# Turning tiles by blocks on a trip through device memory instead of on TensorE

## The chip, the cores and the metric

The kernel runs on one core of a Trainium2 chip. The metric is the device time of one execution in microseconds; lower is better. A core has five engines that run their own instruction streams in order: TensorE (PE in the profile; its weight loads are listed as PEld), VectorE (DVE), ScalarE (ACT), GpSimd (POOL) and SyncE (SP). In this kernel SP issues all DMAs. The engines wait for each other through semaphores.

## The reference

The input is x of 4 sequences of 512 tokens with 512 features. Two blocks are added to it one after the other.

The first is gated linear attention with 4 heads of 128 on the normalised x:

```python
x = x + attn(layernorm(x))
# attn, by chunks of 128 tokens and by heads:
#   k = k / max(norm(k), 1e-12)
#   decay[c, e] = exp(cla[c] - cla[e]) where e <= c, else 0
#   scores = (q @ k.T) * beta * decay ;  y_local = scores @ v
#   y = y_local + (q @ state) * exp(cla)
#   state = state * exp(cla_end) + (k * beta * exp(cla_end - cla)).T @ v
x = x + ffn(layernorm(x))
# ffn: weights of 4 bits with a scale for 32 values,
#   gate = h @ Wg.T ; up = h @ Wu.T ; out = (gelu(gate) * up) @ Wd.T
```

All of it is in fp32. In the second block the kernel splits each fp32 operand into a high and a low part and a mixed one, and multiplies the three parts.

## The kernel before, in words

A tile is 128 tokens by 512 features in fp32, one row to a partition: 256 KB. A sequence has 4 tiles (n = 0 to 3), each of them also a chunk of the attention, so chunks run from (0,0) to (3,3). TensorE contracts over partitions, so a normalised tile must be turned (features onto partitions) before it is multiplied with weights, and so must k before the scores.

The program is a list of steps p. For each sequence b there are 12: four products of v (`product_v`), four of q, four of k. After each product `behind(p)` issues other work by p modulo 3, and by it a chunk of the attention takes three steps, 9 steps behind its sequence: chunk 4b+n begins at p = 9 + 3(4b+n).

- p%3 == 0: `chunk_lead` (kT, the turned k, into which ScalarE copies the bank), `chunk_decay` (exponentials on ScalarE, masks and products on GpSimd, the next load of sums, `load_sums`).
- p%3 == 1: `turn("f")` and `turn("a")` turn what the second and the first norm have left over; then `chunk_scores`: the scores `sp` out of kT and q, and VectorE's product with the decay (L597). Then the loads of x and of xr, the residual.
- p%3 == 2: `chunk_sums`: `dp` and `yp`, then VectorE's residual sum (L649); then `rest`: GpSimd's `chunk_values`, `second_norm` of the chunk and the sum of the state; then `first_norm` of a tile of the next sequence; then `settle`, which normalises what is waiting (L312, `hn_f` and `hn_a`).

`norm` takes the statistics on VectorE, the power -0.5 on GpSimd (`rs`), and defers the rest to `settle`. `turn` makes four TensorE transposes of 128x128 into a PSUM bank (L333) and calls `use`: for the first norm ScalarE copies the bank into hT, the input of the products; for the second ScalarE makes the high part (L356), VectorE the low and the mixed one (L357, L358), and three stores bring them to device memory, from where the second block loads them.

The order is written out by hand: each engine runs its instructions in the order in which these functions issue them, and so does SP with its DMAs. From step 13 on, a slot of `unpack` (VectorE's conversion of the 4-bit weights) follows each step with p%3 of 1 or 2. The second block begins at step 46 and drives the remaining chunks from inside its own products. The functions that the diff touches, and `turn`, which it no longer uses for some tiles, are below. `one_k` hands out the SBUF places of 2 KB a partition and takes them back.

Of the kernel before, what the change touches and what calls it, by code (L numbers as in the profile page):

```python
# [8 lines left out]
F32 = mybir.dt.float32  # L9
# [4 lines left out]
AF = mybir.ActivationFunctionType  # L14
ALU = mybir.AluOpType
# [6 lines left out]
P = 128  # L22
# [13 lines left out]
def f32(t):  # L36
    return t.bitcast(F32)
# [3 lines left out]
def tile_gated_linear_attention__then__nvfp4_geglu(  # L41
# [19 lines left out]
    nc = tc.nc  # L61
    B, T, D = x.shape
    H = D // P
    NCH = T // P
    NT = B * NCH
    KC = D // P
# [59 lines left out]
    def heads(t):  # L126
        return t.rearrange("p (h d) -> p h d", d=P)

    def bc(a):
        return a.unsqueeze(2).to_broadcast([P, a.shape[1], P])  # L130
# [161 lines left out]

    settled, turned = [], []

    def norm(src, key, use, parts=1, within=None):

        st = small.tile([P, 6], F32, tag="st", name=f"st_{key}")
        nc.vector.bn_stats(st, f32(src))
        if within:
            within()  # L300
        mv = small.tile([P, 2], F32, tag="mv", name=f"mv_{key}")
        nc.vector.bn_aggr(mv, st)
        rs = small.tile([P, 1], F32, tag="rs", name=f"rs_{key}")
        nc.vector.tensor_scalar(rs, mv[:, 1:2], 1e-5, None, ALU.add)
        nc.gpsimd.tensor_tensor(rs, rs, minus_half[:, :1], ALU.pow)

        def settle():

            hn = one_k.get(f"hn_{key}")
            w = D // parts  # L310
            for cols in (slice(i * w, (i + 1) * w) for i in range(parts)):
                nc.vector.tensor_scalar(  # L312
                    f32(hn)[:, cols].rearrange("p (c two j) -> p c two j", two=2, j=P),
                    f32(src)[:, cols].rearrange("p (c j two) -> p c two j", two=2, j=P),
                    mv[:, 0:1], rs, ALU.subtract, ALU.mult,
                )
            one_k.put(src)
            turned.append((hn, key, use))

        settled.append(settle)  # L320
# [6 lines left out]
    def turn(which, most=NT):  # L327
        for done in [t for t in turned if t[1][0] in which][:most]:
            turned.remove(done)
            hn, key, use = done  # L330
            tp = psum(f"tp_{key}")
            for k in range(KC):
                nc.tensor.transpose(tp[:, k * P : (k + 1) * P], f32(hn)[:, k * P : (k + 1) * P], ident)  # L333
            one_k.put(hn)
            use(tp)

    def first_norm(b, n, src, within=None):
        if n == 0:
            hT[b] = [two_k.get(f"hT{b}_{c}") for c in range(KC // 2)]

        soon = b == n == 0

        def use(tp):
            for c in range(KC // 2):
                to = f32(hT[b][c])[:, :, n * P : (n + 1) * P]
                new = tp[:, 2 * c * P : 2 * (c + 1) * P].rearrange("p (two t) -> p two t", two=2)
                for part in ((0, 1), (1, 2)) if soon else ((0, 2),):
                    nc.scalar.copy(to[:, slice(*part), :], new[:, slice(*part), :])

        norm(src, f"a{b}_{n}", use, 2 if soon else 1, within)  # L350

    def second_norm(b, n, src):
        def use(tp):
            g = [one_k.get(f"g{j}_{b}_{n}") for j in range(3)]
            hi, lo, mi = g
            nc.scalar.activation(hi, tp, AF.Copy, scale=HI)  # L356
            nc.vector.tensor_tensor(lo, tp, f32(hi), ALU.subtract)  # L357
            nc.vector.scalar_tensor_tensor(mi, f32(hi), ONE_E, tp, ALU.mult, ALU.subtract)  # L358
            for j in range(3):
                nc.sync.dma_start(  # L360
                    h2d[b][j][:, :, n * P : (n + 1) * P].rearrange("k p t -> p k t"), heads(f32(g[j]))
                )
            one_k.put(*g)

        norm(src, f"f{b}_{n}", use)


    zs, ss = {}, {}
# [25 lines left out]
    def product_q(b, h):  # L394
# [10 lines left out]
            f32(q_sb[b][h // 2])[:, h % 2, :], pq, AF.Identity, bias=bq_sb[:, h : h + 1]  # L405
        )

    def product_k(b, n):

        pk = psum(f"pk_{b}_{n}")  # L410
        for k in range(KC):
            nc.tensor.matmul(  # L412
                pk, f32(hT[b][k // 2])[:, k % 2, n * P : (n + 1) * P], f32(wk[k // 2])[:, k % 2, :],
                start=(k == 0), stop=(k == KC - 1),
            )
        kt = one_k.get(f"k_{b}_{n}")
        k_sb[b, n] = kt
        nc.vector.tensor_tensor(f32(kt), pk, f32(bk_sb), ALU.add)
        return lambda: k_factors(b, n, kt)

    def k_factors(b, n, kt):
        sq = one_k.get(f"sq_{b}_{n}")
        sn = small.tile([P, H], F32, tag="ss", name=f"ss{b}_{n}")
        for h in range(H):
            hs = slice(h * P, (h + 1) * P)
            nc.scalar.activation(
                f32(sq)[:, hs], f32(kt)[:, hs], AF.Square, accum_out=sn[:, h : h + 1]
            )
        one_k.put(sq)
        nc.gpsimd.tensor_scalar(sn, sn, 1e-24, None, ALU.max)  # L430
        nc.gpsimd.tensor_tensor(sn, sn, minus_half, ALU.pow)
        brn = small.tile([P, H], F32, tag="brn", name=f"brn{b}_{n}")
        nc.gpsimd.tensor_tensor(brn, sn, beta[b][:, n * H : (n + 1) * H], ALU.mult)
        kwf = small.tile([P, H], F32, tag="kwf", name=f"kwf{b}_{n}")
        nc.gpsimd.tensor_tensor(kwf, sn, bdte[b][:, n * H : (n + 1) * H], ALU.mult)
        ss[b, n] = brn, kwf
# [76 lines left out]
    state, ch = {}, {}  # L513

    def chunk_lead(b, n):
        kT = one_k.get(f"kT_{b}_{n}")
        tp = psum(f"tpk_{b}_{n}")
        for h in range(H):
            nc.tensor.transpose(  # L519
                tp[:, h * P : (h + 1) * P], f32(k_sb[b, n])[:, h * P : (h + 1) * P], ident  # L520
            )
        nc.scalar.copy(f32(kT), tp)
        ch["kT"] = kT
# [38 lines left out]
    def chunk_values(b, n):  # L562

        brn, kwf = ss.pop((b, n))
        kt = k_sb[b, n]
        if n + 1 < NCH:
            kw = one_k.get(f"kw_{b}_{n}")
            nc.gpsimd.tensor_tensor(heads(f32(kw)), heads(f32(kt)), bc(kwf), ALU.mult)
            ch["kw"] = kw
        vb = one_k.get(f"vb_{b}_{n}")  # L570
        ch["vb"] = vb
        if b < B - 1:
            nc.gpsimd.tensor_tensor(heads(f32(vb)), heads(f32(v_sb[b, n])), bc(brn), ALU.mult)
        else:
            for h in range(H):
                hs = slice(h * P, (h + 1) * P)
                nc.scalar.activation(
                    f32(vb)[:, hs], f32(v_sb[b, n])[:, hs], AF.Copy, scale=brn[:, h : h + 1]
                )
# [91 lines left out]
    def chunk_of(p):  # L671
        b, n = divmod((p - 2 * NCH - 1) // 3, NCH)
        return (b, n) if 0 <= b < B else None
# [24 lines left out]
    def behind(p):  # L698
        place[0] = p + 1
        b, j = divmod(p, 3 * NCH)  # L700
        chunk = chunk_of(p)
        first = b < B
        if not first:
            between_steps(p)
        left = chunk if p not in met else None
        if p % 3 == 0:
            if left:
                chunk_lead(*chunk)
            exps = gates_exp(b) if first and j == 3 else None
            if chunk and chunk[1] == 0:  # L710
                chunk_values(*chunk)
            if first and j == 6:
                exps = gates_sums(b)
            if left:
                chunk_decay(*chunk)
            if exps:
                exps()
        elif p % 3 == 1:
            turn("f")

            if p > 1:
                turn("a")
            if left:
                chunk_scores(*chunk)
            if first and j == 7:
                gates_end(b)
                load_sums(b, 0)
            for t in early.get(p + 4, ()):
                if t[0] > 1:
                    xs[t] = load(tile_of(t[0] * NCH + t[1]), f"x{t[0]}_{t[1]}")  # L730
            t = (p - 2 * NCH - 2) // 3 + 1
            if 0 <= t < NT:
                acc[divmod(t, NCH)] = load(tile_of(t), f"xr{t}")
        else:
            if first and j == 5:
                gates_ln(b)
            if chunk and not summed:
                sums, rest = chunk_sums(*chunk)
                sums()
                summed.append(rest)  # L740
            while summed:
                summed.pop()()
            for t in early.get(p, ()):
                first_norm(*t, xs.pop(t))
            if p + 1 < 3 * NCH * B:
                settle()
# [173 lines left out]
    with tc.manual_schedule():  # L920
# [45 lines left out]
        p = 0  # L966
# [95 lines left out]
```

## Time and profile before

| | us |
|---|---|
| median of 3 runs | 1308.09 (1307.48 to 1310.34) |
| the profiled execution | 1308.09, span 1306.1 |
| PE busy | 1296.4 (99%) |
| VectorE busy | 954.0 (73%) |
| ScalarE busy | 461.5 (35%) |
| GpSimd busy | 108.9 (8%) |

The attention with its products takes the first 225 us or so; the last chunks lie between the first products of the second block. The page gives busy time by engine, then groups of instructions by line. A row such as `L357 TENSOR_TENSOR g<-tp_f,g` is named by the line of the kernel and by the tiles written and read. In a timeline the bracket at the end of a row tells how long the engine stood idle before it, and what ended that. The chain is followed back from the last instruction, and its pieces can be listed in order of time. In a list of windows each row gives the stretch, its length, the busy time of PE, PEld, DVE, ACT and POOL with the number of instructions in brackets, the clock granted to TensorE (1.00 is full), the DMA share and GB/s.

### The profile page before, as it was taken

The page shows a single profiled execution, that of the slowest core. Times are in us where ns is not written, and L with a number is a line of the kernel's source. Part 1 is how long each engine was busy: PE and PEld are TensorE (multiplying, and loading weights), DVE is VectorE, ACT ScalarE, POOL GpSimd, SP SyncE. Part 2 cuts the span into 40 slices and gives each one's busy share as a digit, 9 for nine tenths or more (in the row PEclk, how much of TensorE's full clock was granted, in tenths as well). Part 3 has the DMA queues.
Part 4 walks back from the last instruction along what each step waited for, and adds up shares of the span by engine and source line. Part 5 has one row for each costly group of instructions (what it writes and reads, how often), then busy time and mean ns, then how long its engine had stood idle before and what let it go on. Part 6 is the DMA issues. An engine that isn't in the chain of part 4 may idle for free.

```text
span 1306.1 us, 17024 instructions
## 1 busy us (share of the span) xinstructions
PE 1296.4 (99%) x5808; PEld 1038.3 (79%) x5808; DVE 954.0 (73%) x1539; ACT 461.5 (35%) x908; POOL 108.9 (8%) x179
## 2 busy tenths in 40 slices
PE   9999999999999999999999999999999999999998
PEld 6677676778888888888888888888888888887886
DVE  3467665798777777777777777777777777777566
ACT  2443435753333333333333333333333333332332
POOL 1535263410000000000000000000000000000000
PEclk9999999999999999999999999999999999999999
DMA  5235446888555555555555555555555555555463
GB/s 194 82 108 173 123 128 211 266 272 261 184 184 187 187 185 183 187 186 184 185 186 186 186 187 184 186 184 187 183 186 186 188 183 186 185 177 197 169 248 128
DMA packets 176374, 240.79 MB, mean 184 GB/s; under 512 B 16096, under 2 KB 74784, under 8 KB 176288
## 3 DMA queue, kind: packets, MB, share of 16 engines
q1 hardware_dynamic: 176288, 239.72, 56.7%
q8 instruction: 45, 0.74, 0.2%
q14 instruction: 41, 0.34, 0.1%
HBM read 187.19 MB, written 52.46 MB: 183 GB/s over the span
## 4 chain that ended last, share of the span: by engine, by line
PE 96%; DMA 2%; DVE 2%; ACT 1%; issue 0%; SPq 0%; POOL 0%; DVEq 0%; ACTq 0%; POOLq 0%
PE pa L774 35%; PE p_d L818 26%; PE pb L774 17%; PE pq L400 4%; PE pk L412 4%; PE pva L375 2%; PE pvb L382 2%; PE sp L586 1%; PE yp L640 1%; PE dp L611 1%; DMA x<-h 1%; PE yp L642 1%; PE tp_a L333 1%; PE tp_f L333 0%; PE tpk L519 0%; DMA h<-g 0%
## 5 line engine op out<-in xcount | busy, mean ns | idle before, releaser
L774 PE MATMUL pa<-x,wgu 128*128 128x512 f32 x2048 | 507.1, 390 | 0.0
L774 PEld LDWEIGHTS pa<-x,wgu 128*128 128x128 f32 x2048 | 383.9, 188 | 79.0
L818 PE MATMUL p_d<-wd,i 128*128 128x512 f32 x1542 | 357.3, 390 | 2.3 <-DVE xr L649 0.6
L818 PEld LDWEIGHTS p_d<-wd,i 128*128 128x128 f32 x1542 | 288.4, 188 | 65.7 <-DVE i L798 2.1
L779 ACT ACTIVATE t<-pb 128x512 f32<-128x512 f32 x256 | 151.2, 591 | 358.9 <-PE pb L774 355.5
L774 PE MATMUL pb<-x,wgu 128*128 128x512 f32 x1024 | 275.3, 390 | 1.5 <-DMA x<-h 1.4
L780 DVE TENSOR_TENSOR t<-pa,t 128x512 f32<-128x512 f32 x256 | 176.5, 690 | 82.6 <-ACT t L779 76.9
L774 PEld LDWEIGHTS pb<-x,wgu 128*128 128x128 f32 x1024 | 192.3, 188 | 43.0 <-DMA x<-h 3.2
L826 DVE SCALAR_TENSOR_TENSOR acc<-p_d,acc 128x512 f32<-128x512 f32 (+1 forms) x137 | 93.4, 682 | 124.4 <-PE p_d L818 123.9
L794 ACT ACTIVATE i<-t 128x512 fp32r<-128x512 f32 x128 | 81.0, 633 | 194.2 <-DVE t L791 191.2
L786 ACT ACTIVATE t<-t 128x512 f32<-128x512 f32 x128 | 81.1, 634 | 135.8 <-DVE t L780 135.7
L798 DVE TENSOR_TENSOR i<-t,i 128x512 fp32r<-128x512 f32 x128 | 88.4, 690 | 25.9 <-ACT i L794 24.1
L830 DVE TENSOR_TENSOR acc<-acc,p_d 128x512 f32<-128x512 f32 x135 | 92.9, 688 | 14.1
L791 DVE SCALAR_TENSOR_TENSOR t<-t,t 128x512 f32<-128x512 f32 x128 | 88.6, 692 | 4.3
L799 DVE SCALAR_TENSOR_TENSOR i<-i,t 128x512 fp32r<-128x512 f32 x128 | 88.1, 689 | 0.0
L849 POOL TENSOR_TENSOR acc<-acc,last 128x512 f32<-128x512 f32 x1 | 1.3, 1295 | 1015.1 <-ACT last L848 1015.1
L400 PE MATMUL pq<-hT,wq 128*128 128x512 f32 x128 | 57.7, 595 | 0.0
L412 PE MATMUL pk<-wk,hT 128*128 128x512 f32 x128 | 57.4, 593 | 0.0
L400 PEld LDWEIGHTS pq<-hT,wq 128*128 128x128 f32 x128 | 23.3, 191 | 23.5 <-issue 23.4
L412 PEld LDWEIGHTS pk<-wk,hT 128*128 128x128 f32 x128 | 23.2, 191 | 23.4 <-issue 23.4
L183 DVE TENSOR_TENSOR wgu<-wgu,wgu 128x1024 fp32r<-128x1024 f32 x32 | 39.0, 1218 | 0.0
L171 DVE SCALAR_TENSOR_TENSOR w_gu<-i_gu,sc_gu 128x1024 f32<-128x1024 f16 x32 | 38.9, 1216 | 0.0
(117 smaller groups left out, 913.7 us busy)
## 6 DMA issues: line engine op xcount, KB each, us to landing
x<-h SPq DMA_DIRECT2D x420, 256.0 KB
acc<-acc SPq DMA_DIRECT2D x256, 256.0 KB
h<-g SPq DMA_DIRECT2D x48, 256.0 KB
x<-in_x SPq DMA_DIRECT2D x16, 256.0 KB
pk_gu<-in_gate_p SPq DMA_DIRECT2D x32, 128.0 KB
sc_gu<-in_gate_s SPq DMA_DIRECT2D x64, 64.0 KB
pk_gu<-in_up_p SPq DMA_DIRECT2D x32, 128.0 KB
sc_gu<-in_up_s SPq DMA_DIRECT2D x64, 64.0 KB
```

What stands on the lines that cost most here:

```text
L400: nc.tensor.matmul(pq, f32(wq[k // 2])[:, k % 2, h * P : (h + 1) * P], f32(hT[b][k // 2])[:, k % 2, :], start=(k == 0), stop=(k == KC - 1),)
L412: nc.tensor.matmul(pk, f32(hT[b][k // 2])[:, k % 2, n * P : (n + 1) * P], f32(wk[k // 2])[:, k % 2, :], start=(k == 0), stop=(k == KC - 1),)
L774: nc.tensor.matmul(o, w3[j][:, k % 2, c * P : (c + 1) * P], x[j * KC + k], start=(j == js[0] and k == 0), stop=(j == js[-1] and k == KC - 1),)
L779: nc.scalar.activation(f32(t), pb, AF.Copy, scale=-1.0 / ONE_E)
L780: nc.vector.tensor_tensor(f32(t), pa, f32(t), ALU.add)
L786: nc.scalar.activation(f32(g), f32(g), AF.Gelu_apprx_tanh, scale=ONE_E)
L791: nc.vector.scalar_tensor_tensor(f32(u), f32(g), ONE_E, f32(u), ALU.mult, ALU.mult)
L798: nc.vector.tensor_tensor(il, f32(u), f32(ih), ALU.subtract)
L799: nc.vector.scalar_tensor_tensor(im, f32(ih), ONE_E, f32(u), ALU.mult, ALU.subtract)
L818: nc.tensor.matmul(banks[key_][:, part], inter[i][j][:, n * P : (n + 1) * P], wd[ms[i] // 2][j][:, ms[i] % 2, part], start=(i == 0 and j i ...
L826: nc.vector.scalar_tensor_tensor(a, banks[n, False, part.start][:, part], ONE_E, a, ALU.mult, ALU.add)
L830: nc.vector.tensor_tensor(a, a, banks[n, True, 0], ALU.subtract)
```

## The change

27 tiles are turned in another way: the first norm's of sequences 1 to 3 (12), the second norm's of sequences 0 and 1 (8), and k of the chunks for which `far` holds: 0 < n and 4b+n < 10, that is (0,1) to (0,3), (1,1) to (1,3) and (2,1) (7).

Such a tile is written with its columns regrouped (`crossed`): blocks of 32 columns that will go to the same 32 partitions stand together. `cross` stores it into device memory in one DMA with runs of 512 bytes. `land` loads it back in four DMAs of 64 KB each, in such an order that each 32x32 block stands in the partitions where it belongs, but not yet turned. `turn_blocks` then turns all its 32x32 blocks on VectorE, straight into hT, into kT, or into a new tile h2T; in the last case `use` makes the three parts out of SBUF instead of PSUM.

The places in the order: the store follows the normalisation in `settle` (p%3 == 2) or the addition of k's bias; the loads of norm tiles are issued at the start of the next `behind` with p%3 == 0, the loads of a k at the p%3 == 1 two steps ahead of its chunk. The turn of norm tiles, and for the second norm its split and stores, stand at p%3 == 2 three steps after the store, between `rest` and `first_norm`. The turn of k stands in `chunk_lead`, where its transposes were. The normalisation of such tiles is done in two instructions of 256 columns, and the bias, the squares and the factor kw of k use the regrouped columns.

```diff
+    def cross(src, key, use):
+        way = dram.tile([KC, P, P], F32, tag=f"way_{key}", name=f"way_{key}")
+        nc.sync.dma_start(way.rearrange("w p m -> p w m"), f32(src).rearrange("p (w m) -> p w m", m=P))
+        return way, key, use
+
+    def land(way, key, use):
+        t = one_k.get(f"way_{key}")
+        for a in range(KC):
+            nc.sync.dma_start(f32(t)[:, a * P : (a + 1) * P], way[:, a * 32 : (a + 1) * 32, :])
+        return lambda: use(t)
+
+    def turn_blocks(t, *to):
+
+        new = f32(t).rearrange("p (a k i) -> p k a i", a=KC, i=32)
+        done = 0
+        for part in to:
+            n = part.shape[1]
+            nc.vector.transpose(part.rearrange("p k (a j) -> p k a j", j=32), new[:, done : done + n])
+            done += n
+        one_k.put(t)
...
+            if way:
+                for c in range(2):
+                    nc.vector.tensor_scalar(
+                        crossed(f32(hn)).rearrange("p (c two) w i -> p c two w i", c=2)[:, c],
+                        f32(src).rearrange("p (c w i two) -> p c two w i", c=2, w=KC, two=2)[:, c],
+                        mv[:, 0:1], rs, ALU.subtract, ALU.mult,
+                    )
+                one_k.put(src)
+                coming.append(cross(hn, key, way))
+                one_k.put(hn)
+                return
...
-        norm(src, f"a{b}_{n}", use, 2 if soon else 1, within)
+        def way(t):
+            turn_blocks(t, *(f32(hT[b][c])[:, :, n * P : (n + 1) * P] for c in range(KC // 2)))
+
+        norm(src, f"a{b}_{n}", use, 2 if soon else 1, within, way if b > 0 else None)
...
-        norm(src, f"f{b}_{n}", use)
+        def way(t):
+            hT2 = one_k.get(f"h2T_{b}_{n}")
+            turn_blocks(t, heads(f32(hT2)))
+            use(f32(hT2))
+            one_k.put(hT2)
+
+        norm(src, f"f{b}_{n}", use, way=way if b < 2 else None)
...
-        nc.vector.tensor_tensor(f32(kt), pk, f32(bk_sb), ALU.add)
+        nc.vector.tensor_tensor(heads_of(kt, far(b, n)), in_blocks(pk), in_blocks(f32(bk_sb)), ALU.add)
+        if far(b, n):
+            ways[b, n] = cross(kt, f"k{b}_{n}", lambda t: turn_blocks(t, heads(f32(ch["kT"]))))
...
     def chunk_lead(b, n):
+        if far(b, n):
+            ch["kT"] = one_k.get(f"kT_{b}_{n}")
+            ways.pop((b, n))()
+            return
...
         if p % 3 == 0:
+            come.extend(land(*t) for t in coming)
+            coming.clear()
...
         elif p % 3 == 1:
+            after = chunk_of(p + 2)
+            if after and far(*after):
+                ways[after] = land(*ways[after])
...
             while summed:
                 summed.pop()()
+            while come:
+                come.pop(0)()
             for t in early.get(p, ()):
                 first_norm(*t, xs.pop(t))
```

More of the change, by code (lines that the diff above doesn't have):

```diff
@@ L293, in tile_gated_linear_attention__then__nvfp4_geglu, with crossed, norm @@
     settled, turned = [], []
-    def norm(src, key, use, parts=1, within=None):
+    coming, come = [], []
+    def crossed(t):
+        return t.rearrange("p (w k i) -> p k w i", w=KC, i=32)
+    def cross(src, key, use):
[15 more added lines that the diff above has]
+        one_k.put(t)
+    def norm(src, key, use, parts=1, within=None, way=None):
         st = small.tile([P, 6], F32, tag="st", name=f"st_{key}")
@@ L406, in product_q, with far, in_blocks, heads_of @@
         )
+    def far(b, n):
+        return 0 < n and NCH * b + n < 2 * NCH + 2
+    ways = {}
+    def in_blocks(a):
+        return a.rearrange("p (h w i) -> p h w i", h=H, i=32)
+    def heads_of(t, blocks):
+        return crossed(f32(t)) if blocks else in_blocks(f32(t))
     def product_k(b, n):
@@ L426, in k_factors @@
             nc.scalar.activation(
-                f32(sq)[:, hs], f32(kt)[:, hs], AF.Square, accum_out=sn[:, h : h + 1]
+                f32(sq)[:, hs].rearrange("p (w i) -> p w i", i=32), heads_of(kt, far(b, n))[:, h],
+                AF.Square, accum_out=sn[:, h : h + 1],
             )
@@ L567, in chunk_values @@
             kw = one_k.get(f"kw_{b}_{n}")
-            nc.gpsimd.tensor_tensor(heads(f32(kw)), heads(f32(kt)), bc(kwf), ALU.mult)
+            nc.gpsimd.tensor_tensor(
+                in_blocks(f32(kw)), heads_of(kt, far(b, n)),
+                kwf.unsqueeze(2).unsqueeze(3).to_broadcast([P, H, KC, 32]), ALU.mult,
+            )
             ch["kw"] = kw
```

## The prediction

> **What bounds the kernel now.** First the page: who is busy, and which chain ends last.
>
> ```profile
> PE 1296.4 (99%) x5808; PEld 1038.3 (79%) x5808; DVE 954.0 (73%) x1539; ACT 461.5 (35%) x908; POOL 108.9 (8%) x179
> ...
> PE 96%; DMA 2%; DVE 2%; ACT 1%; issue 0%; SPq 0%; POOL 0%; DVEq 0%; ACTq 0%; POOLq 0%
> ```
>
> PE is busy nearly from end to end, so whatever leaves PE is worth its full time, unless PE then waits. The second view is the chain in order of time over one attention cycle (three steps of the program, here the steps 24 to 26 with chunk (1,1)); columns are start, length, what.
>
> ```profile
> 116.72 1.78 PE pva L375 x8
> 118.51 1.73 PE pvb L382 x8
> 120.23 0.44 PE tpk L519 x4
> 120.67 1.78 PE pva L375 x8
> 122.45 1.73 PE pvb L382 x8
> 124.18 0.44 PE tp_f L333 x4
> 124.61 0.44 PE tp_a L333 x4
> 125.05 0.89 PE sp L586 x8
> ```
>
> No gap: a turned tile costs 0.44 us of chain, and the scores (sp) start 8.3 us after the chunk before ended (yp, 116.72). The third view is VectorE's rows in that stretch. The reader is to see that it starts at the same moment, released by yp, and has 6.7 us of rows before it is through with step 24.
>
> ```profile
> 116.76 0.69 DVE L649 TENSOR_TENSOR xr<-xr,yp 128x512 f32<-128x512 f32 x1 [1.09 <-PE yp L640]
> ...
> 120.12 0.55 DVE L312 TENSOR_SCALAR hn_f<-xr,mv_f,rs_f 128x512 f32<-128x512 f32 x1
> 121.11 0.55 DVE L312 TENSOR_SCALAR hn_a<-x,mv_a,rs_a 128x512 f32<-128x512 f32 x1 [0.45 <-POOL rs_a L305]
> 121.57 1.22 DVE L171 SCALAR_TENSOR_TENSOR w_d<-i_d,sc_d 128x1024 f32<-128x1024 f16 x1
> 122.71 0.42 DVE L390 TENSOR_TENSOR v<-pva,bv 128x264 f32<-128x264 f32 x1
> ...
> 123.45 0.42 DVE L390 TENSOR_TENSOR v<-pva,bv 128x264 f32<-128x264 f32 x1
> ```
>
> Today this backlog costs nothing: the scores need kT, which goes PE (tpk), ScalarE (L522), and never passes VectorE. The change puts kT behind it.
>
> **What leaves PE.** First norm, sequences 1 to 3: 12 tiles; second norm, sequences 0 and 1: 8; k of chunks (0,1) to (0,3), (1,1) to (1,3), (2,1): 7. 27 x 0.44 = 11.9 us. Nothing else hides behind these transposes, so alone the change would give 1308.1 - 11.9 = 1296.2. ScalarE loses two copies of 0.37 for a first-norm tile and one of 0.58 for a kT; at 35% busy that is worth nothing.
>
> **What VectorE gets, and where.** Start to start, a 512-wide one-result row takes 0.60 (L357, then L358). The block turn is in no row of before. Low end 0.46 (the normalising row, 121.11 to 121.57), high end 1.13 (the 1024-wide L171, 121.57 to 122.71); I take 0.60, the plain row of its width, and 0.33 for each half, two to a first-norm tile. The other rows:
>
> ```profile
> 125.34 0.69 DVE L357 TENSOR_TENSOR g<-tp_f,g 128x512 fp32r<-128x512 f32 x1 [0.64 <-ACT g L356]
> 125.95 0.68 DVE L358 SCALAR_TENSOR_TENSOR g<-g,tp_f 128x512 fp32r<-128x512 f32 x1
> ...
> 5.37 0.74 DVE L312 TENSOR_SCALAR hn_a<-x,mv_a,rs_a 128x256 f32<-128x256 f32 x2
> ```
>
> In step p%3==2, behind the sums and ahead of the norms and the unpacking, now stand: the second-norm turn 0.60; the wait for ScalarE's hi, which needs that turn (0.59 for L356 and two hand-overs: 0.75; low 0.6, high 1.5 if ScalarE is behind); lo and mi 1.20, moved here from p%3==1; the first-norm turn 0.66. Normalising in two pieces is 0.65 by the pair above (5.37 to 6.02) instead of 0.46: +0.2 a tile, twice, less 0.2 of the wait for rs_a that the longer hn_f covers. Then, in step p%3==0, the kT turn 0.60, and 0.13 for its end and the hand-over. Together 2.55 + 0.66 + 0.2 + 0.73 = 4.15 us on top of what VectorE has there now. The k add with a strided result, and the squares, stay at today's price: they read and write as many elements; the squares are off the chain.
>
> **Where it turns into PE time.** PE wants each of the seven scores 1.32 earlier (three transposes gone; 0.88 for the last). VectorE's free time is read from its rows as above, the scores' start from the chain:
>
> (0,1): VectorE free at 62.07; no second norm yet but two first-norm tiles, so +2.25 = 64.3; scores wanted 64.83 - 1.32 = 63.5; wait 0.8.
> (0,2): 78.07 + 4.15 = 82.2 against 80.16 - 1.32 = 78.85; 3.4.
> (0,3): 93.19 + 4.15 = 97.35 against 96.32 - 1.32 = 95.0; 2.3.
> (1,1): 123.45 + 4.15 = 127.6 against 125.05 - 1.32 = 123.75; 3.85.
> (1,2): 138.84 + 4.15 = 143.0 against 140.39 - 1.32 = 139.05; 3.9.
> (1,3): 153.34 + 4.15 = 157.5 against 156.54 - 1.32 = 155.2; 2.3.
> (2,1): 181.34 + 4.15 = 185.5 against 184.84 - 0.88 = 183.95; 1.55.
>
> Sum 18.1. Behind the waiting scores PE has the next product, dp and yp (7 us), and VectorE only some 3 us of rows, so VectorE is idle again at the next yp and every cycle starts clean; the waits add. The product of step p%3==1 is ahead of the scores and hides nothing that is not counted. In the other cycles kT still goes by ScalarE; there dm (L597) is VectorE's next debt: in the cycle of (1,0) the same sum has it done by 113.0, and yp wants it near 114.8, so nothing. Net: 18.1 - 11.9 = +6.2.
>
> With the ends: every term low (0.46 for 0.60, 0.25 for a half, 0.6 for the wait, 1.05 for lo and mi, hn at no extra) takes 1.1 from six of the waits and 0.5 from the first: 11 remain, net -1. All high (1.13, 0.6 a half, 1.5) adds 2.35 to six and 1.6 to the first: 34, net +22.
>
> The VectorE page of the Trainium skill (VectorE: DVE Perf Modes, "The three transpose paths" and "Rules for kernel authors") speaks against the change: for 128x128 it sends one to TensorE, and it lists 311 ns for a VectorE turn of 128 columns. No row here shows that; by its figure a 512-wide turn is an estimated 1.24, some 1.9 us more in each of seven cycles, and the time 1332 instead of 1319.4.
>
> **The clock.** All seven waits are longer than any that PE has now in mid-run (0.79 at 273.8). The end of the trace shows what idleness does: PE's last matmul ends at 1302.13, and the granted clock falls to 0.5 about 2.1 us later.
>
> ```profile
> 1302.00:1303.00 1.00, 0.12 (x2) 0.00 (x0) 0.90 (x3) 0.00 (x0) 0.00 (x0) 1.00 0.04 10
> 1304.00:1305.00 1.00, 0.00 (x0) 0.00 (x0) 0.00 (x0) 0.00 (x0) 0.00 (x0) 0.58 0.60 201
> ```
>
> At the start nine products of 128 columns take 4.21 us for their 18 passes, 0.234 each, where a turned tile now takes 0.44 for four, 0.11 each: half pace, and it lasts at most from 1.52 to 7.30, where the first long product runs at its usual length. So a fall may cost up to half of 5.8, 2.9 us; low end nothing. Five waits are over 2.1 us, three over 3. I take a fall for these three, 1.7 us each, a little above the middle since the waits come back every cycle: 5.1. High end five times 2.9, 14.5.
>
> TensorE: Matmul & The Clock Gate of the Trainium skill ("Why this matters for your kernels") warns of PE gaps over some 3 us, with half rate after. No wait of that length is in this trace. By it the three longest waits would count and the time is 1319.4; by a trace without a fall in mid-run it is 1314.3.
>
> **DMA and the queues.** Each tile adds a write of 256 KB and four reads of 64 KB, all issued by SP. An h<-g issue takes 0.37, so some 5.5 us of SP in a cycle of 15 to 18, where SP mostly waits. SP is in order: the landing waits for its write, and load_sums and the xr and x loads stand behind it; these are wanted a step to a cycle later. Traffic: 27 x 0.52 = 14.2 MB in some 155 us, +91 GB/s on the 122 of 30 to 177 us, where the DMA share is 0.42; in proportion 0.73. Writing starts when hn is done, 7 to 8 us after yp; by the 5.2 us that a store and the 5.5 that a load take in the late chain, the tile is in by 18 or 19, and VectorE wants it at 20 or later. Cost nothing; if that cover of 2 us is gone, VectorE stops for the lateness and PE with it: 1 to 3 us in six cycles, +6 to +18.
>
> **Sum.** The profiled execution took 1308.09 with a span of 1306.1; that is also the median, so nothing is to be translated. 1308.1 + 6.2 + 5.1 = 1319.4.
>
> **Rivals.**
> 1. Waits without a fall of the clock: 1314.3. For it: PE is fully loaded before and after each wait, and only the end of the kernel shows a fall. Against it: that fall came 2.1 us after work that was just as dense.
> 2. Gain, the other side: VectorE's extra rows fit in the gap after yp, and kT comes in time. Against it: at (1,1) and (1,2) the rows leave 1.6 us, 0.3 once PE comes 1.32 earlier. For it: all 4.15 rests on rows of other operations. It decides once the additions average under some 3.2 us, where the waits sum to 11.9. No wait at all: 1296.2; half of them: 1305.
> 3. A tie: all terms at the low end and no fall, 1306 to 1310.
> 4. Landings late or slow block turns: PE's waits double, 1325 to 1337.
> That the change doesn't do what it says is no rival: the turned tiles' path has no PE call left.
>
> **How the numbers follow.** My forecast 0.46, rival 1 0.24, rival 2 0.10, rival 3 0.08, rival 4 0.12. A difference under 0.2% (2.6 us) is not told from none. Slower 0.82, same 0.08, faster 0.10. Range 1305 to 1332: below it lies rival 2, above it the end of rival 4. The forecast alone: 1314 to 1325.
>
> **What would show it.** tp_a down to 16 transposes, tp_f to 32, tpk to 36. PE idle before sp (L586) released by VectorE's turn of kT, seven times, 1 to 4 us; VectorE waiting for ScalarE's hi in p%3==2; matmuls near double length after the longer waits, PEclk under 1 there; the MLP unchanged but shifted. Wrong if sp waits for nothing, if VectorE waits for a landing, or if a 512-wide turn is far from 0.6.

## The result, and the profile after

The changed kernel takes 1352.88 us (median of 4 runs, 1352.05 to 1354.7) against 1308.08 (1307.48 to 1310.34): a ratio of 1.0341, with a 95% interval of 1.0323 to 1.0359. It is 44.8 us slower, where 11 were forecast. The profiled span went from 1306.1 to 1351.8 us, and the mean granted clock from 0.999 to 0.982. One execution of e1 below, at a granted clock of 0.556 from end to end, is in no figure.

From the page of the changed kernel, the engines' busy time, the share of each in the chain that ended last, and the granted clock in 40 slices of the span:

```profile
PE 1304.5 (97%) x5700; PEld 1038.4 (77%) x5700; DVE 980.5 (73%) x1598; ACT 451.7 (33%) x877; POOL 109.3 (8%) x179
...
PEclk9879888999999999999999999999999999999999
...
PE 83%; DMA 7%; SPq 4%; DVE 4%; issue 1%; ACT 1%; POOL 1%; DVEq 0%; POOLq 0%; ACTq 0%
```

PE lost 108 instructions, the 27 x 4 transposes, and yet its busy time rose: 1284.5 would have been left (1296.4 - 11.9), so some 20 us went to a lower pace, all of it in the attention stage (mean granted clock 0.90 over the first 250 us, 1.00 after). PE's share of the chain fell from 96% to 83%, and DMA and SP's queue, which had 2% and 0%, now have 11% together. The reader should stop at that figure: transfers and their issues became part of what sets the end.

PE's rows in order of time, those of the scores with a wait ahead of them (start, length, what, and in brackets the idle time and what ended it):

```profile
72.75 2.04 PE L658 MATMUL sp<-q,kT 128*128 128x128 f32 x8 [4.96 <-DVE kT L320]
...
94.65 2.04 PE L658 MATMUL sp<-q,kT 128*128 128x128 f32 x8 [4.70 <-DVE kT L320]
...
115.25 1.13 PE L658 MATMUL sp<-q,kT 128*128 128x128 f32 x8 [3.28 <-DVE ncla L561]
...
152.38 2.05 PE L658 MATMUL sp<-q,kT 128*128 128x128 f32 x8 [8.27 <-DVE kT L320]
...
174.23 1.95 PE L658 MATMUL sp<-q,kT 128*128 128x128 f32 x8 [5.20 <-DVE kT L320]
...
194.45 1.71 PE L658 MATMUL sp<-q,kT 128*128 128x128 f32 x8 [3.48 <-DVE ncla L561]
...
229.33 2.05 PE L658 MATMUL sp<-q,kT 128*128 128x128 f32 x8 [2.40 <-DVE kT L320]
```

These are the seven waits of the forecast, at the places named: chunks (0,1) to (0,3), (1,1) to (1,3) and (2,1). They sum to 32.3 us instead of 18.1. (Where ncla is named, kT's turn had ended 0.14 us before the scores, as in the others.) The scores take up to 2.05 us, where such a row took 1.06 before. With 2.79 of idleness ahead of dp, 2.62 ahead of tp_f and 0.24 ahead of yp, PE idles 38.0 us: 38.0 + 20 - 11.9 = 46, the span's 45.7.

The chain in order of time over a cycle, that of chunk (1,1); it is the stretch in which, before, PE's pieces stood without a gap:

```profile
132.06 5.04 DMA way_f<-hn_f
...
137.12 0.56 SPq L311
...
141.20 5.15 DMA way_a<-way_a
...
146.48 0.77 DVE hT L320 x2
...
149.00 0.74 DVE hn_a L343 x2
...
151.61 0.63 DVE kT L320
...
152.25 4.60 DMA way_f<-hn_f
```

No PE piece is left. The chain is the trip itself: a store to DRAM (5.0 us), eight landing issues by SP (4.1, of which the first is shown), the last landing (5.2), the turn, VectorE's rows behind it, and the next store. VectorE's rows in that cycle:

```profile
137.13 0.69 DVE L721 TENSOR_TENSOR xr<-xr,yp 128x512 f32<-128x512 f32 x1
...
143.08 0.71 DVE L320 STREAM_TRANSPOSE h2T<-way_f 128x512 f32<-128x512 f32 x1 [3.53 <-DMA way_f<-way_f]
144.54 0.69 DVE L401 TENSOR_TENSOR g<-h2T,g 128x512 fp32r<-128x512 f32 x1 [0.74 <-ACT g L400]
...
146.48 0.77 DVE L320 STREAM_TRANSPOSE hT<-way_a 128x256 f32<-128x256 f32 x2 [0.65 <-DMA way_a<-way_a]
...
148.15 0.73 DVE L343 TENSOR_SCALAR hn_f<-xr,mv_f,rs_f 128x256 f32<-128x256 f32 x2
...
151.52 0.71 DVE L320 STREAM_TRANSPOSE kT<-way_k 128x512 f32<-128x512 f32 x1
```

The turn of 512 columns takes 0.71 us, the two halves 0.77, the wait for ScalarE's hi 0.74 and the normalising pair 0.73: the forecast's terms of VectorE hold. What it has not is the 3.53 us for which VectorE stands still for the landing of way_f. SP's issues in the same cycle:

```profile
132.06 1.20 SPq L305 DMA_DIRECT2D way_f<-hn_f  x1
133.35 0.78 SPq L305 DMA_DIRECT2D way_a<-hn_a  x1
134.22 0.82 SPq L305 DMA_DIRECT2D way_k<-k  x1
137.12 2.28 SPq L311 DMA_DIRECT2D way_f<-way_f  x4
139.51 2.71 SPq L311 DMA_DIRECT2D way_a<-way_a  x4
142.27 0.66 SPq L573 DMA_DIRECT2D sums<-rows  x1
...
143.45 3.55 SPq L311 DMA_DIRECT2D way_k<-way_k  x4
...
149.50 2.65 SPq L404 DMA_DIRECT2D h<-g  x3
152.25 0.94 SPq L305 DMA_DIRECT2D way_f<-hn_f  x1
```

Four landings take SP 2.28 to 3.55 us, and the cycle from one store of way_f to the next is 20.2 us long. From 132.06 to 152.25 SP issues for 16.7 us and waits 2.1 more, from 135.04 to 137.12, for the store's end. The "SP mostly waits" of the forecast is no longer so. The last part of the cycle is SP's too: hn_f is through at 148.88, and its store leaves at 152.25, right behind three issues of h<-g, though the chain names VectorE's kT and v there.

### The profile page after: what moved, and what is told of

The parts are those of the page before. It is cut to its first block, busy times and chain, and to the rows that moved or that the text cites. A ratio compares the mean times of both kernels' runs of the same rounds, so it can differ in the third digit from the quotient of the medians.

```text
span 1351.8 us, 17039 instructions
## 1 busy us (share of the span) xinstructions
PE 1304.5 (97%) x5700; PEld 1038.4 (77%) x5700; DVE 980.5 (73%) x1598; ACT 451.7 (33%) x877; POOL 109.3 (8%) x179
## 4 chain that ended last, share of the span: by engine, by line
PE 83%; DMA 7%; SPq 4%; DVE 4%; issue 1%; ACT 1%; POOL 1%; DVEq 0%; POOLq 0%; ACTq 0%
PE pa L853 34%; PE p_d L897 25%; PE pb L853 17%; SPq L311 3%; PE pq L450 2%; DMA way_f<-hn_f 2%; DMA way_a<-way_a 2%; PE pk L474 1%; DMA way_k<-way_k 1%; PE pva L425 1%; DMA x<-h 1%; PE pvb L432 1%; PE sp L658 1%; SPq L201 1%; DMA x<-in_x 0%
## 5 line engine op out<-in xcount | busy, mean ns | idle before, releaser
L877 DVE TENSOR_TENSOR i<-t,i 128x512 fp32r<-128x512 f32 x128 | 88.3, 690 | 25.9 <-ACT i L873 24.1
L474 PE MATMUL pk<-wk,hT 128*128 128x512 f32 x128 | 60.2, 617 | 0.0
L658 PE MATMUL sp<-q,kT 128*128 128x128 f32 x128 | 22.5, 332 | 32.3 <-DVE kT L320 25.5
L658 PEld LDWEIGHTS sp<-q,kT 128*128 128x128 f32 x128 | 20.5, 238 | 38.7 <-issue 38.0
L450 PEld LDWEIGHTS pq<-hT,wq 128*128 128x128 f32 x128 | 24.6, 199 | 25.5 <-issue 25.3
```

The source lines that it names most:

```text
L450: nc.tensor.matmul(pq, f32(wq[k // 2])[:, k % 2, h * P : (h + 1) * P], f32(hT[b][k // 2])[:, k % 2, :], start=(k == 0), stop=(k == KC - 1),)
L474: nc.tensor.matmul(pk, f32(hT[b][k // 2])[:, k % 2, n * P : (n + 1) * P], f32(wk[k // 2])[:, k % 2, :], start=(k == 0), stop=(k == KC - 1),)
L877: nc.vector.tensor_tensor(il, f32(u), f32(ih), ALU.subtract)
```

## The experiments

Two theories were set against each other at first: that kT behind VectorE's rows is the whole price (with the clock), and that the trip through DRAM closes a loop of its own. All runs stand beside runs of the kernel before on their own chip; ratios are to those, with 95% intervals.

| run | what | median us | ratio | interval |
| --- | --- | --- | --- | --- |
| change | | 1352.88 | 1.0341 | 1.0323-1.0359 |
| e1 | change, PE's waits filled | 1352.59 | 1.0336 | 1.0308-1.0364 |
| e2 | no trip | 1330.77 | 1.0168 | 1.0144-1.0192 |
| e5 | no trip, waits filled | 1320.80 | 1.0085 | 1.0066-1.0103 |
| e3 | without k | 1328.30 | 1.0152 | 1.0129-1.0174 |
| e9 | without the second norm | 1323.09 | 1.0107 | 1.0093-1.0120 |
| e4 | turns behind the scores, landings early | 1345.97 | 1.0284 | 1.0261-1.0307 |
| e6 | as e4, no trip | 1303.08 | 0.9950 | 0.9931-0.9969 |
| e8 | eight landings a tile instead of four | 1436.99 | 1.0964 | 1.0939-1.0990 |
| e10 | turns behind the scores, landings late | 1331.83 | 1.0180 | 1.0165-1.0196 |
| e12 | as e10, four of the seven k | 1315.39 | 1.0049 | 1.0033-1.0066 |
| e7 | as e10, no k | 1302.37 | 0.9943 | 0.9926-0.9960 |
| e11 | as e7, first norm ahead of the scores | 1311.88 | 1.0026 | 1.0017-1.0036 |

**e1: is it the clock?** PE gets idle products of the identity ahead of the scores, about as long as its waits.

```diff
+        if far(b, n):
+            fill = psum(f"fill_{b}_{n}")
+            for _ in range((0, 20, 20, 14, 0, 34, 22, 14, 0, 10)[NCH * b + n]):
+                nc.tensor.matmul(fill[:, :P], ident, ident, start=True, stop=True)
```

> Ahead of the scores of the seven chunks whose k is turned by blocks, PE gets idle products of 128x128 (20, 20, 14, 34, 22, 14 and 10 of them, about 0.22 us each) into a bank that nobody reads, so that it works through most of the wait it has there. Theory A (a fall of the clock after the waits costs some 20 us: PE's busy time rose by 8 us although 108 transposes of 0.11 us left it): the granted clock stays near 1.00 and the time falls from 1352.9 to 1333 to 1338. Rival: the long matmuls after the waits have another reason, and the waits just move: 1350 to 1356.

The granted clock rose from 0.982 to between 0.993 and 0.996 in the three timed runs, and the time stayed: 1352.59 (1351.11 to 1355.15). The 20 us of lower pace in the changed kernel cost nothing of their own. That a PE that is done earlier then waits longer for the same kT fits this; no trace of e1 at a full clock shows its waits.

**e2: is it the trip?** Store and landing go; the turn reads the tile that is in SBUF. The result is then not a transpose across blocks; everything else stays.

```diff
     def cross(src, key, use):
-        way = dram.tile([KC, P, P], F32, tag=f"way_{key}", name=f"way_{key}")
-        nc.sync.dma_start(way.rearrange("w p m -> p w m"), f32(src).rearrange("p (w m) -> p w m", m=P))
-        return way, key, use
+        return src, key, use
 
     def land(way, key, use):
-        t = one_k.get(f"way_{key}")
-        for a in range(KC):
-            nc.sync.dma_start(f32(t)[:, a * P : (a + 1) * P], way[:, a * 32 : (a + 1) * 32, :])
-        return lambda: use(t)
+        return lambda: use(way)
...
```

> Leaves out the store to device memory and the four loads of every such tile; VectorE turns the blocks of the tile as it stands in SBUF, so blocks don't reach their partitions and the values are others. All of VectorE's work and its places stay. Theory A (the order on VectorE: kT stands behind the second norm's turn, split and wait): the waits of 3 to 5 us at chunks (0,2), (0,3), (1,2), (1,3) stay, and only the lateness of landings at (0,1), (1,1) and (2,1) goes (about 9 us of waits and a part of the clock): 1330 to 1340. Rival B (the trip itself, SP's issue of 0.5 us a load and 5 us a transfer, is the cost): 1300 to 1315. Rival C (landings don't matter): 1350 to 1354.

1330.77, the low end of the range under theory A: the trip is worth 22.1 us, and most of the waits stay. PE's rows of this kernel, three of the seven waits:

```profile
61.94 1.13 PE L653 MATMUL sp<-q,kT 128*128 128x128 f32 x8 [0.76 <-DVE kT L315]
...
132.32 2.05 PE L653 MATMUL sp<-q,kT 128*128 128x128 f32 x8 [3.94 <-DVE kT L315]
...
154.66 2.05 PE L653 MATMUL sp<-q,kT 128*128 128x128 f32 x8 [5.24 <-DVE kT L315]
```

The seven are 0.76, 4.70, 2.37, 3.94, 5.24, 3.53 and 1.29, 21.8 us, where the forecast, which costed the DMA at nothing, had 0.8, 3.4, 2.3, 3.85, 3.9, 2.3 and 1.55. Without the trip its waits come within 1.4 us of every one, and PE's busy time is 1295.5, 11 over 1284.5.

**e5: the clock where PE is in the loop.** e2 with fills of 2, 20, 10, 17, 22, 14 and 5 products.

```diff
...
+            for _ in range((0, 2, 20, 10, 0, 17, 22, 14, 0, 5)[NCH * b + n]):
+                nc.tensor.matmul(fill[:, :P], ident, ident, start=True, stop=True)
```

> Without the trip (store and loads left out, so the values are others) and with idle products of 128x128 on PE ahead of the scores (2, 20, 10, 17, 22, 14 and 5 of 0.22 us). In the kernel without the trip PE idled 21.8 us before the scores and was busy 11 us more than 1296.4 - 11.9. Theory (without the trip the cycle runs through PE, so a slow PE after each wait costs): PE's clock stays up and the time falls by 8 to 11 us to 1320 to 1323. Rival (as in the kernel with the trip, the clock is not in the loop): 1329 to 1332.

1320.80, at a clock of 0.998 to 1.0: 10.0 us less than e2, the 11 of lower pace nearly in full. A like fill is worth nothing in e1 and ten microseconds here. The two together say that the clock's price depends on who sets the cycle: PE and VectorE without the trip, the trip with it.

**e3: is it k behind VectorE?** k's transposes go back to PE, the norms stay.

```diff
     def far(b, n):
-        return 0 < n and NCH * b + n < 2 * NCH + 2
+        return False
```

> k is turned by TensorE and copied by ScalarE again in all chunks; the norms' 20 tiles still make the trip and are turned on VectorE in the same place. Theory A (the cost arises because kT stands behind the other work on VectorE): the scores wait for nothing, 20 x 0.44 = 8.8 us of PE are saved, 1299 to 1303. Rival B (the trips and the added work of VectorE cost by themselves, whoever makes kT): 1320 or more.

1328.30, not 1299 to 1303. With kT off VectorE the price should have been gone, and half of it stayed; this fells the first theory. The chain of this kernel in order of time:

```profile
66.82 0.77 DVE hT L320 x2
...
68.57 0.66 DVE hn_f L343 x2
69.25 2.35 DMA way_f<-hn_f
71.61 0.53 SPq L311
...
76.46 4.82 DMA way_a<-way_a
81.47 0.77 DVE hT L320 x2
...
83.22 0.66 DVE hn_f L343 x2
83.89 3.50 DMA way_f<-hn_f
...
92.17 4.83 DMA way_a<-way_a
97.13 0.77 DVE hT L320 x2
```

This is a closed loop, without PE, at 14.65 and 15.66 us a turn. PE meets it through the other engines: its longest wait here, 5.67 us ahead of the scores at 134.69, is for ScalarE's copy of kT, which stands behind ScalarE's hi, which waits for the late turn. The turn of one cycle's tiles stands on VectorE ahead of the normalising of the next (both in step p%3==2), so: turn, statistics and normalising 2.4 us, store, eight issues on SP some 4.9, landing 4.8, turn. A late landing makes the next store late by the same amount, and nothing gives it back. With k's store and four landings in SP's order the loop is 20.2 us (above).

**e9: the second norm.** First norm and k turned, the second norm's tiles by PE.

```diff
-        norm(src, f"f{b}_{n}", use, way=way if b < 2 else None)
+        norm(src, f"f{b}_{n}", use)
```

> Only the first norm's tiles and k go by blocks, in the places of the change; the second norm's 8 tiles stay on TensorE. Theory (order and loop): VectorE's chain ahead of kT is shorter by 2.55 us, and SP has four loads and a store fewer in a cycle, so the loop is near PE's cycle of 14 to 15 us. Waits remain where two first-norm tiles come together (chunks (0,0) and (0,1), 7 to 8 us) and under 1 us at (0,2), (1,1), (1,2); 19 x 0.44 = 8.4 us are gained and 2 to 5 lost to the clock: 1306 to 1318. Rival (first norm and k alone carry the loss): 1340 or more.

1323.09, above the expected range. The part that this kernel leaves to PE adds 29.8 us to the change, k's part adds 24.6 (e3) and the trip 22.1 (e2); they sum to more than the whole, as they would if they are links of one loop and each, taken out, shortens it.

**e4: the turn behind the scores.** The turns move one step back, to p%3==1 behind the scores; the landings stay where they were issued.

```diff
         if p % 3 == 0:
+            ready.extend(come)
+            come.clear()
             come.extend(land(*t) for t in coming)
...
             if left:
                 chunk_scores(*chunk)
+            while ready:
+                ready.pop(0)()
...
-            while come:
-                come.pop(0)()
```

> All 27 tiles as in the change, but the turn of the norms' tiles, the split and the stores stand in p%3==1 behind the scores, five steps after the store instead of three; only the turn of kT and the two-piece normalising remain between yp and the scores. Theory A: the waits shrink to 0 to 1 us in each of the seven, landings are in time, the clock stays, and most of the 11.9 us are gained: 1296 to 1302. Rival B (the work on VectorE as such is too much, or the trips are the cost): 1320 or more.

1345.97, not 1296 to 1302. The waits of this kernel (total, times, longest):

```profile
ACT dm L603 <- DMA sums<-rows: 55.9, 7, 16.3
...
DVE kT L320 <- DMA way_k<-way_k: 20.4, 4, 7.6
```

VectorE no longer stands behind the landings of the norms, but SP does: the landing waits in SP's queue for its store, and the loads of sums and k's landings behind it are late now, and with them dm and kT (20.4 and 2.3 us of such waits in the change).

**e6: the same without the trip.** e4 and e2 together: the turns behind the scores, store and landing left out.

> The trip left out (values are others) and the norms' turn moved to p%3==1 behind the scores, five steps after the normalisation. Theory (two causes, the order on VectorE and the trip, and no third): waits of 0 to 1 us before the scores remain, 11.9 us are gained: 1296 to 1301. Rival (the added work on VectorE is itself too much): over 1306.

1303.08, PE's busy time 1285.0, which is before less the 11.4 for the transposes (11.9 forecast); 4.6 us of waits for kT are left, so it is a little above the expected range. By themselves neither the order (e4: -6.9) nor the trip (e2: -22.1) carries the price; both taken away give 49.8 back.

**e8: SP's issues.** Each landing in eight pieces of 32 KB instead of four of 64 KB: same bytes, twice the issues.

```diff
         for a in range(KC):
-            nc.sync.dma_start(f32(t)[:, a * P : (a + 1) * P], way[:, a * 32 : (a + 1) * 32, :])
+            for w in (0, 2):
+                nc.sync.dma_start(
+                    f32(t)[w * 32 : (w + 2) * 32, a * P : (a + 1) * P],
+                    way[w : w + 2, a * 32 : (a + 1) * 32, :],
+                )
```

> The change with each landing issued as eight DMAs of 32 KB in place of four of 64 KB, same bytes and same runs of 512. Theory (SP's serial issue of 0.55 us a landing is in the loop): 12 more issues in a cycle with f, a and k, 2.2 us for each tile, 4.4 to 6.6 us a cycle over some eight cycles: 1380 to 1400. Rival (only the transfers' latency and VectorE's order count): 1350 to 1358.

1436.99, more than the 1380 to 1400 expected. The waits ahead of the same seven scores sum to 89.4 us instead of 32.3; two of PE's rows:

```profile
84.94 2.04 PE L662 MATMUL sp<-q,kT 128*128 128x128 f32 x8 [14.46 <-DVE kT L324]
...
197.85 2.05 PE L662 MATMUL sp<-q,kT 128*128 128x128 f32 x8 [21.12 <-DVE kT L324]
```

Summed over the trace, the 216 landing issues take SP 154.3 us (0.71 each) and the 108 of the change 69.5 (0.64 each): 84.8 us more of SP, and 84.1 us more of time. The transfers on the chain are not longer: way_f's stores take 4.7 to 5.4 us there, 4.6 to 5.5 in the change. It is the number of issues in SP's order, not the bytes, that is on the path. Why an issue of half the size is not shorter was not tried.

**e10, e7 and e12: the landing late too.** The landings are issued at the end of p%3==1, behind the loads of x and xr, when most of their stores are done; the turns come a cycle later, behind the scores. e10 does so with all 27 tiles, e7 with the 20 of the norms (far returns False), e12 with these and k of the chunks with n of 2 and 3 in sequences 0 and 1 (far: 1 < n).

```diff
         if p % 3 == 0:
-            come.extend(land(*t) for t in coming)
-            coming.clear()
...
             if left:
                 chunk_scores(*chunk)
+            while come:
+                come.pop(0)()
...
+            come.extend(land(*t) for t in coming)
+            coming.clear()
         else:
...
-            while come:
-                come.pop(0)()
```

> All 27 tiles, complete computation; order and landings of the norms' tiles as in the run without k (landing at the end of p%3==1, turn behind the scores a cycle later). Theory: the norms' tiles cost no wait; kT still stands behind norms and unpacking on VectorE, so the waits of the run without the trip and with the moved turn (1.3 to 1.9 us at four places) come back, and 11.9 us are gained: 1301 to 1306; above that if k's landing, two steps ahead of its turn, is late behind SP's other issues. Rival (k by blocks costs as much as in the change): 1320 or more.

> Complete computation: the 20 tiles of the norms make the trip, k stays on TensorE. Landings are issued at the end of p%3==1, two steps after the store and behind the loads of x and xr; the turn stands in p%3==1 behind the scores, a whole cycle after the landing. Theory (the cost was a loop, turn, normalise, store, SP's issues, load, that is longer than PE's cycle, and the order on VectorE): with a cycle in hand the loop is open, nothing waits, 20 x 0.44 = 8.8 us gained: 1298 to 1302. Rival (SP and the DMA engines can't carry it in 14 us a cycle): 1312 or more.

> The complete computation with late landings for the norms' 20 tiles, and k by blocks only for (0,2), (0,3), (1,2), (1,3), which have two or more steps between store and landing. With k of seven chunks the time was 1331.8, without k 1302.4; 11.4 us of the waits before the scores stood at the three chunks with n = 1. Theory (k's trip is late where it has one step, and SP's twelve more loads and stores a cycle delay the rest): 1306 to 1318. Rival (only n = 1 is at fault): 1300 to 1304, 1.8 us of transposes gained less waits of 1 to 2 us.

e7 takes 1302.37 (1301.54 to 1302.7), 0.4 over its expected range, 6 us (0.6%) less than the kernel before, with an interval wholly below 1. Its page and the waits of PE that are left:

```profile
PE 1287.6 (99%) x5728; PEld 1029.8 (79%) x5728; DVE 970.8 (75%) x1591; ACT 455.7 (35%) x884; POOL 109.4 (8%) x179
```

```profile
64.30 2.02 PE L425 MATMUL pva<-wva,hT 128*128 128x264 f32 x8 [1.30 <-DVE hT L320]
...
128.70 2.05 PE L425 MATMUL pva<-wva,hT 128*128 128x264 f32 x8 [1.26 <-DVE hT L320]
...
161.84 0.66 PE L588 MATMUL tpk<-ident,k 128*128 128x128 f32 x4 [0.67 <-DVE k L480]
```

Twenty turned tiles are worth 20 x 0.44 = 8.8 us of PE, and PE's busy time fell by just that, 1296.4 to 1287.6; 3.2 us of it go to these three waits. The trip is that of the change, with 100 of its 135 issues: it costs next to nothing once a tile has a whole cycle more to make it. Against e3, which has the same 20 tiles with turn and landing in the change's places, the later places are worth 25.9 us. k takes this away again. In e10 (1331.83 instead of 1301 to 1306) SP waits 10.7 us for way_k's stores and ScalarE 25.8 for the sums behind them; k of n = 1 has one step between store and landing. But e12 leaves these out, its k have three and five steps, and with 24 tiles it is still 13 us over e7, inside its range. Its SP rows show what is short: SP's own time. The pauses between issues that are longer than 0.3 us sum to 84.0 us from 60 to 180 us in the kernel before, to 17.5 in e7 (60 to 175) and to 4.5 in e12 (60 to 180). That the full queue alone makes the 13 us was not tested apart.

**e11: an attempt at more.** e7 with the first norm's turns ahead of the scores, to take the two pva waits away.

```diff
+            first_come = [c for c in come if c[0][0] == "a"]
+            for c in first_come:
+                come.remove(c)
+                c[1]()
             if left:
                 chunk_scores(*chunk)
```

> The 20 tiles of the norms with late landings, k on TensorE, and the first norm's turn ahead of the scores' product with the decay, the second norm's behind it. The run without k had two waits of 1.3 us of the v product for VectorE's turn of hT, which stood behind that product. Theory: these go, 1299 to 1301.5. Rival: the product with the decay becomes late and yp waits: 1302 to 1306.

1311.88, 9.5 us worse than e7 and over both ranges. From its view of waits, and one of PE's rows:

```profile
DVE hT L320 <- DMA way_a<-way_a: 27.6, 9, 4.5
```

```profile
129.89 0.80 PE L712 MATMUL yp<-vb,dm 128*128 128x128 f32 x2 [3.40 <-DVE dm L669]
```

A few rows earlier the turn comes before its landing, and dm, which stands behind it on VectorE, keeps yp waiting.

## Why the prediction was wrong

- **The transposes, 11.9 us:** right. PE lost 108 instructions, and e6's busy time is 11.4 lower.
- **VectorE's terms, 4.15 us a cycle:** right in kind and nearly in size. The turn measured 0.64 start to start (0.60 taken), the pair of halves 0.69 (0.66), hi 0.70 to 0.78 (0.75). The estimate of 1.24 from the Trainium skill (VectorE: DVE Perf Modes, "The three transpose paths") would have been worse: its 311 ns is for 128x128 in bf16, and does not multiply by four for these fp32 turns of 512 columns. The advice of the same page ("Rules for kernel authors") to use TensorE for a 128x128 turn agrees with the change as it was made, 44.8 us slower, and not with e7, 6 us faster.
- **The waits, 18.1 us:** right only without the trip (e2: 21.8). With it 32.3. The sentence "VectorE is idle again at the next yp and every cycle starts clean; the waits add" failed: a late landing makes the next store late (e3's chain).
- **The clock, 5.1 us:** too small where it counts (10.0, e5 against e2), though within its bound of 14.5, and nothing in the change itself (e1). The rule of the Trainium skill (TensorE: Matmul & The Clock Gate, "Why this matters for your kernels") that gaps of over some 3 us halve the rate agrees with e2: after a wait of 3.94 the scores took 2.05 us, after one of 0.76 they took 1.13. As a sharp bound it does not hold here: in the change, tp_f took 1.09 instead of 0.60 after a wait of 2.62, with the granted clock at 0.50 from 226 to 232 us, and the scores took 1.13 after one of 3.28. Whether the pace is on the path is another question (e1, e5).
- **"DMA and the queues", cost nothing: this is the step that failed.** It took 0.37 for each issue, "some 5.5 us of SP in a cycle of 15 to 18, where SP mostly waits", and put the tile at 18 or 19 us after yp where VectorE wanted it at 20 or later. A landing's issue took 0.51 to 1.31 us (medians 0.52 for way_f, 0.56 for way_a, 0.73 for way_k); in the cycle shown, the turned tiles' issues alone took SP 12.1 us instead of 5.5, and all issues 16.7 of 20.2. And the sum of the trip, 7 or 8 and 5.2 and 5.5, has no term for the issues between store and last landing: they took 4.1 us, and way_a was in 23.0 us after the residual sum at 123.34, while VectorE stood ready for its first turn 16.2 us after it. The text itself had the bound, "if that cover of 2 us is gone … +6 to +18", and the runs give 22.1 (e2). What it had no eye for is that the path from store to landing closes on itself through the orders of VectorE and SP: a cover of 2 us, used up once, is not renewed.
- **"In the other cycles … nothing":** failed at (1,0). Without a wait its cycle from xr to xr is 13.8 us (123.34 to 137.13), too short for the trip of the tiles in it, and the longest wait, 8.27, is that of the next scores.

The sum by its own steps: 1319.4, and 3.7 for waits, some 5 for the clock and 22.1 for the trip make 1350 of 1352.9. The rest of 2.7 us lies in e2, which is 11.4 over 1319.4, and was not traced to one cause. Rival 4, "Landings late or slow block turns", with 1325 to 1337 was the nearest; its first half is what happened, at 16 us over its upper end.

## What to carry to other kernels

Before a tile is sent through DRAM inside a pipelined loop, write the round trip down as a cycle (store, every issue on its queue at the length that rows of that form have, landing, whatever stands ahead of the next store) and compare its length with the loop's own period: where the trip is the longer one, its lateness is handed on from cycle to cycle, and a cover of a few us does not stop it. If the tile can wait, move landing and use a whole cycle later rather than a few rows (e7 against e3: 25.9 us with the same 20 tiles). Add up the issuing queue's time as well, and leave on the old path what no longer fits into it (here k). And before a lower clock is priced, ask whether the engine is in the loop: a like fill gave 10 us in one kernel and none in the other.

## What the runs showed beside this

- In the change a landing of 64 KB took 0.51 to 1.31 us of SP's time, a store of 256 KB 0.36 to 1.24. What lengthens an issue was not tested.
- VectorE's normalising pair took 1.44 us and the unpacking's integer row 1.21 (0.73 and 0.69 are usual) while GpSimd ran its products with the state. VectorE's rows and then GpSimd's, of the change at chunk (0,2):

```profile
90.58 1.44 DVE L343 TENSOR_SCALAR hn_a<-x,mv_a,rs_a 128x256 f32<-128x256 f32 x2
91.94 1.21 DVE L167 TENSOR_SCALAR i_gu<-i_gu 128x1024 int32<-128x1024 int32 x1
```

```profile
91.12 1.48 POOL L616 TENSOR_TENSOR qc<-q,cd 128x256 f32<-128x256 f32 x2
92.57 1.48 POOL L626 TENSOR_TENSOR state<-state,td 128x512 f32<-128x512 f32 x1
```

GpSimd's state product is longer too (1.04 at the median), its pair qc hardly (1.41 before). Only the coincidence was seen; it was not tried apart.
